# Spreading weight preparation over the steps of a Strassen matmul kernel, and loading the first rows as whole 128-row tiles

## The chip, the cores and the metric

The kernel runs on one core of one Trainium2 chip. The metric is device time in microseconds (us), median over the runs of one kernel.

## The reference, cut to what matters

Two layers of attention over a graph. Each multiplies the tokens `h` by three 768 x 768 matrices (left, right, lin) of that layer:

```python
h = jnp.maximum(_layernorm(x, axis=-1), 0.0)
for l in range(L):                                   # L = 2
    m_left  = jnp.einsum('bsh,oh->bso', h, W_left[l])
    m_right = jnp.einsum('bsh,oh->bso', h, W_right[l])
    u_left  = jnp.einsum('bih,bjh->bij', h, m_left) / temper
    u_right = jnp.einsum('bih,bjh->bij', h, m_right) / temper
    ...                                              # masked exp of u, rows normalized: attention
    h_lin = jnp.einsum('bsh,oh->bso', h, W_lin[l]) + b_lin[l]
    ctx = jnp.matmul(attention, h_lin)
    h = jax.nn.relu(_layer_norm(ctx, ln_a[l], ln_b[l]))
return x + h
```

`x` is 128 x 64 x 768 in float32: 16 blocks of 512 tokens.

## The kernel before

Each layer is two passes over the 16 blocks. The first computes left, right and the attention ("scores"), the second lin and the context. The products are Strassen's: seven in place of eight, with sums of weight quarters (S1 to S4) and of token quarters (T1 to T4) prepared by VectorE or GpSimd. One product is a *step*: three float32 matmuls, which the trace shows as six, into one of the PSUM banks X, Y, Z and V, the tiles that matmuls write and that VectorE or ScalarE then reads. In the profiles, ts are the token sums, wm the masks or (beside w_n) its means, and aux takes the transposes of the first rows, the scores and the context. A block of the first pass is 42 steps and one group of scores.

Every other engine's work is put into a queue, and one item is taken after each step. So a place in the queue is a place in time, and an empty item (a "blank") moves all that follows by one step. The order on each engine is fixed when the program is built. Cuts are marked with "..."; some short lines are joined.

```python
queue = deque()
def pump(n):
    for _ in range(min(n, len(queue))):
        queue.popleft()()

def centre(l):                       # subtract the column mean from w_n ("lin")
    ...
        queue.append(means)          # four VectorE operations on w_n and a 128x3 tile
        for s in (a, b):
            queue.append(lambda s=s, m=m: nc.gpsimd.tensor_sub(t[s], t[s], ...))

def sums_w(l, kind, eng):            # S1..S4 of one matrix
    ...
        queue.append(lambda ...: getattr(eng, f)(t[o], t[a], t[b]))

def load_rows(l, u, pool, engines=(nc.sync, nc.sync)):
    for g in range(2):
        t = pool.tile([P, 2, H], F32, name="x", bufs=2)
        for a in range(4):           # eight pieces of 32 partitions
            ...
            engines[a % 2].dma_start(t[a * 32:(a + 1) * 32], src.rearrange("(k j) h -> j k h", k=2))

def prepare(u):                      # what block u needs, queued while block u-1 is multiplied
    transpose_rows(l, u, sp)
    queue.append(lambda: load_h(1, l, u))
    if u + 1 < NB:
        queue.append(lambda: load_rows(l, u + 1, sp))
    queue.extend(softmax(u - 2) if u > 1 else [lambda: None] * 6)
    queue.append(lambda: load_adj(u))
    queue.extend([lambda: None] * 6)
    affine(1, l, u)                  # layer 1 only: six ScalarE operations on ht
    queue.append(lambda: masks(u))   # GpSimd, needs adj
    sums_t((1, l, u))                # GpSimd: T1..T4

# pass one, layer 0, before block 0
warm = const.tile(...); nc.scalar.activation(warm, eps_in, AF.Sqrt)   # among the constants
load_rows(0, 0, sp, (nc.sync, nc.scalar)); load_w(0, "l"); load_w(0, "r")
...
sums_w(0, "l", nc.vector)            # interleaved with T1..T4 on VectorE
sums_w(0, "r", nc.gpsimd)
...
for u in range(NB):
    if u == 0:
        queue.extend([lambda: None] * 9)
    ...

def one_aside(l):                    # begun after the first third of a block-1 matrix
    ...                              # in an inner function:
    load_w(l, "n"); bias(l); centre(l); sums_w(l, "n", nc.gpsimd)
```

`bias(l)` loads two rows of `b_lin` and queues six VectorE operations on them (`centred`).

## Time and profile before

| | before |
|---|---|
| median, lowest to highest (6 runs) | 2971.37, 2970.22 to 2975.54 us |
| span of the profiled run | 2970.2 us |
| TensorE busy | 2910.5 us, 98% |
| TensorE idle, all | 59.7 us |

TensorE sets the time: only what it waits for can be won. This is the timeline of the kernel before (start, duration, engine, line, operation, out<-in, count, and in brackets the idle time and what ended it; ACTq is ScalarE's queue of DMA issues):

```profile
0.73 1.28 ACT L163 ACT_TABLE_LOAD   x1 [0.73 <-PEq L654]
...
1.39 0.86 ACTq L189 DMA_DIRECT2D x<-in_x_dram  x2
...
4.53 3.70 ACTq L189 DMA_DIRECT2D x<-in_x_dram  x2
...
14.36 1.02 DVE L175 BATCH_NORM_STATS2 st<-x 128x6 f32<-128x384 f32 x2 [4.42 <-DMA x<-in_x_dram]
```

ScalarE issues two of its four pieces of x at once and the other two only from 4.53 us on. The second half of x is there at 14.36, and the first product waits for it.

### The profile page before, as it was taken

What the parts mean: (1) busy time and instruction counts of PE and PEld (TensorE: products, weight loads), DVE (VectorE), ACT (ScalarE), POOL (GpSimd) and SP (SyncE); (2) the same over time, 40 slices, a digit from 0 to 9 for tenths busy, and PEclk for the clock granted to TensorE, in tenths of its full rate; (3) what the DMA queues carried; (4) which work ended last, traced back from release to release, by engine and by line L of the source; (5) the groups of instructions that cost most, each with busy time, mean ns of one, the idle gap of its engine ahead of it and who ended that gap; (6) DMA issues with size and microseconds to landing.
All of it is one profiled execution on the core that took longest, in us unless ns stands there. A gap on an engine that the chain in (4) does not pass through costs nothing.

```text
span 2970.2 us, 37457 instructions
## 1 busy us (share of the span) xinstructions
PE 2910.5 (98%) x14872; PEld 2246.1 (76%) x14872; DVE 1130.0 (38%) x2312; ACT 582.6 (20%) x1113; POOL 768.2 (26%) x482
## 2 busy tenths in 40 slices
PE   6989999999999999999999999999999999999998
PEld 5878888888888755555588888888888886555554
DVE  5433443334333332222334332333333324555555
ACT  2111211121111122222221111111111112232221
POOL 2132111211121152323223111111111113656564
PEclk9999999999999999999999999999999999999999
DMA  5522234223422153333453342234223303555544
GB/s 152 152 70 70 70 97 108 73 70 91 113 74 70 39 177 101 120 100 121 124 131 107 93 112 73 70 90 114 75 70 83 101 27 114 165 163 149 174 143 133
DMA packets 228719, 310.23 MB, mean 104 GB/s; under 512 B 53696, under 2 KB 179136, under 8 KB 220352
## 3 DMA queue, kind: packets, MB, share of 16 engines
q1 hardware_dynamic: 228224, 307.05, 37.3%
q8 instruction: 117, 1.92, 0.3%
q10 hardware_dynamic: 320, 0.79, 0.1%
q14 instruction: 58, 0.48, 0.1%
HBM read 202.91 MB, written 104.86 MB: 104 GB/s over the span
## 4 chain that ended last, share of the span: by engine, by line
PE 93%; DMA 3%; POOL 2%; SPq 1%; DVE 1%; issue 0%; ACT 0%; DVEq 0%; POOLq 0%; ACTq 0%
PE V L310 16%; PE Z L310 16%; PE X L310 16%; PE Z L543 8%; PE V L543 8%; PE X L543 8%; PE Y L310 8%; PE aux L344 5%; PE Y L543 5%; PE aux L471 3%; DMA x<-in_x_dram 1%; DMA h<-xb 1%; POOL w_n_A L110 1%; POOL w_n_S L118 1%; POOL ts L141 0%; DMA adj<-in_adj_dram 0%
## 5 line engine op out<-in xcount | busy, mean ns | idle before, releaser
L280 POOL TENSOR_TENSOR wm<-adj,tri 128x256 f32<-128x256 f32 x64 | 46.9, 754 | 1401.3 <-DMA adj<-in_adj_dram 1269.7
L141 POOL TENSOR_TENSOR ts<-ht 128x768 f32<-128x768 f32 x126 | 240.0, 1905 | 278.5 <-PE Y L310 157.2
L310 PE MATMUL V<-ts,w_l_A 128*128 128x256 f32 x1152 | 284.4, 383 | 15.3 <-POOL ts L141 11.2
L310 PE MATMUL V<-ts,w_r_A 128*128 128x256 f32 x1152 | 281.4, 380 | 2.2 <-DVE n L331 2.2
L310 PE MATMUL X<-ht,w_l_A 128*128 128x256 f32 x1152 | 282.8, 382 | 0.0
L310 PE MATMUL X<-ht,w_r_A 128*128 128x256 f32 x1152 | 280.3, 379 | 0.0
L543 PE MATMUL X<-w_n_A,ht 128*128 128x384 f32 x768 | 268.8, 486 | 0.0
L543 PE MATMUL V<-w_n_A,ts 128*128 128x384 f32 x768 | 268.6, 486 | 0.0
L329 ACT COPY n<-X 128x256 f32<-128x256 f32 x192 | 71.4, 372 | 1003.9 <-PE X L310 1003.9
L331 DVE TENSOR_TENSOR n<-V,u 128x256 f32<-128x256 f32 x384 | 161.9, 422 | 251.8 <-PE V L310 251.3
L310 PEld LDWEIGHTS V<-ts,w_l_A 128*128 128x128 f32 x1152 | 221.0, 192 | 46.9 <-POOL ts L141 12.0
L310 PEld LDWEIGHTS X<-ht,w_l_A 128*128 128x128 f32 x1152 | 220.9, 192 | 31.2 <-issue 0.6
L310 PEld LDWEIGHTS V<-ts,w_r_A 128*128 128x128 f32 x1152 | 219.6, 191 | 32.5 <-DVE n L331 2.6
L310 PEld LDWEIGHTS X<-ht,w_r_A 128*128 128x128 f32 x1152 | 219.3, 190 | 29.9
L141 POOL TENSOR_TENSOR ts<-ht,ts 128x768 f32<-128x768 f32 x126 | 238.6, 1894 | 5.8 <-issue 3.3
L543 PEld LDWEIGHTS V<-w_n_A,ts 128*128 128x128 f32 x768 | 145.9, 190 | 101.8
L543 PEld LDWEIGHTS X<-w_n_A,ht 128*128 128x128 f32 x768 | 145.8, 190 | 101.6 <-issue 0.3
L497 ACT ACTIVATE z<-aux 128x768 f32<-128x768 f32 x128 | 102.5, 806 | 601.0 <-PE aux L471 586.9
L324 DVE TENSOR_TENSOR u<-Y,s 128x256 f32<-128x256 f32 x192 | 81.6, 425 | 363.3 <-PE Y L310 359.4
L331 DVE TENSOR_TENSOR n<-Z,u 128x256 f32<-128x256 f32 x192 | 81.3, 424 | 306.9 <-PE Z L310 306.8
L327 DVE TENSOR_TENSOR u<-Z,u 128x256 f32<-128x256 f32 x192 | 81.5, 425 | 285.8 <-PE Z L310 285.2
L553 POOL TENSOR_TENSOR u2b<-u,b 128x384 f32<-128x384 f32 x64 | 63.8, 997 | 478.5 <-DVE u L551 465.1
(103 smaller groups left out, 4004.1 us busy)
## 6 DMA issues: line engine op xcount, KB each, us to landing
ht<-h SPq DMA_DIRECT2D x63, 1536.0 KB, 7.1
h<-xb SPq DMA_DIRECT2D x124, 384.0 KB, 6.0
z<-z SPq DMA_DIRECT2D x128, 192.0 KB, 2.9
x<-z SPq DMA_DIRECT2D x128, 192.0 KB, 8.7
xr<-in_x_dram SPq DMA_DIRECT2D x128, 192.0 KB, 3.3
out_dram<-xr SPq DMA_DIRECT2D x128, 192.0 KB, 2.7
x<-in_x_dram SPq DMA_DIRECT2D x124, 192.0 KB, 8.6
adj<-in_adj_dram SPq DMA_DIRECT2D x64, 128.0 KB, 2.8
```

The source lines that it names most:

```text
L141: eng.tensor_sub(b[o], b[m], b[n])
L280: nc.gpsimd.tensor_tensor(WM[u][:, :, k], ADJ[u][:, :, 1 - k], t, op=ALU.mult)
L310: nc.tensor.matmul(p, w[a][:, c, g * P:(g + 1) * P], b[t][:, c, :], start=(new and c == 0), stop=(c == CH - 1), skip_group_check=True)
L324: nc.vector.tensor_add(u2, p, s1)
L327: nc.vector.tensor_add(u4, p, u2)
L329: nc.scalar.copy(to, pb)
L331: nc.vector.tensor_add(to, pb, (u4 if i == 3 else u2).rearrange("p (b s) -> p b s", s=S))
L344: nc.tensor.matmul(p[h * S:(h + 1) * S, q, :], ht[:, c, b * S:(b + 1) * S], m[c // CH][:, c % CH, b].rearrange("p k j -> p (k j)"), start= ...
L471: nc.tensor.matmul(cx[k][i, m, :HH], at[j, q, :], hl[j, q, m * HH:(m + 1) * HH], start=True, stop=True)
L497: nc.scalar.activation(zs[k].rearrange(two, n=2), cx[k], AF.Square, accum_out=ss[:, k:k + 1])
L543: nc.tensor.matmul(p, b[t][:, c, r * P:(r + 1) * P], w[a][:, c, :], start=(new and c == 0), stop=(c == CH - 1), skip_group_check=True)
L553: nc.gpsimd.tensor_add(u2b, u2, rows["b2"])
```

## The change

It is meant to remove the waits of TensorE outside the first loads. A second queue, `idle`, is drawn on only in steps where the first has nothing or a blank. The preparation of w_n goes there, with two blanks ahead of each item, so that token sums on GpSimd come first. The sums of w_r go to VectorE during block 0. The first x is loaded as four whole 128-row tiles ahead of the warming square root.

```diff
+    idle = deque()
+    none = [None]
     def pump(n):
-        for _ in range(min(n, len(queue))):
-            queue.popleft()()
+        for _ in range(n):
+            f = queue.popleft() if queue else None
+            if f is None and idle:
+                f = idle.popleft()
+            if f is not None:
+                f()
 ... in centre: means and tensor_sub
-            queue.append(means)
+            idle.append(means)             # each with idle.extend(none * 2) ahead of it
 ... in bias
-        queue.append(centred)
+        idle.append(centred)
 ... in load_rows, for the first block
+            for g in range(2):
+                t = pool.tile([P, 2, H], F32, name="x", bufs=2)
+                for k in range(2):
+                    engines[k].dma_start(t[:, k, :], rows[0, 2 * g + k])
 ... in prepare
-                queue.extend(softmax(u - 2) if u > 1 else [lambda: None] * 6)
+                queue.extend(softmax(u - 2) if u > 1 else [])
 ... in pass one
-    nc.scalar.activation(warm, eps_in, AF.Sqrt)          # among the constants
                 load_rows(0, 0, sp, (nc.sync, nc.scalar))
+                nc.scalar.activation(warm, eps_in, AF.Sqrt)
-                sums_w(0, "r", nc.gpsimd)
                 if u == 0:
-                    queue.extend([lambda: None] * 9)
+                    queue.extend(none * 4)
+                    if l == 0:
+                        sums_w(0, "r", nc.vector, queue, 1)   # a blank ahead of each
+                    else:
+                        queue.extend(none * 5)
 ... in one_aside
-            sums_w(l, "n", nc.gpsimd)
+            sums_w(l, "n", nc.gpsimd, idle, 2)
```

Left out here: the first rows' new order of tokens in the copy to ht, a loop that empties `idle` after the last block of a pass, and the same blanks written in another way in the second pass.

More of the change, by code (lines that the diff above doesn't have):

```diff
@@ L73, with flush @@
     queue = deque()
+    idle = deque()
+    none = [None]
     def pump(n):
-        for _ in range(min(n, len(queue))):
-            queue.popleft()()
-    def flush(keep=0):
-        pump(len(queue) - keep)
+        for _ in range(n):
[4 more added lines that the diff above has]
+                f()
+    def flush():
+        while queue:
+            pump(1)
     SRC = {"l": w_left, "r": w_right, "n": w_lin}
@@ L100, in centre @@
             m = stat.tile([P, 2, CH], F32, name="wm", bufs=2)
+            idle.extend(none * 2)
             def means(a=a, b=b, m=m):
@@ L106, in means, with sums_w @@
                 nc.vector.tensor_scalar_mul(m[:, 0], m[:, 0], 1.0 / H)
-            queue.append(means)
+            idle.append(means)
             for s in (a, b):
-                queue.append(lambda s=s, m=m: nc.gpsimd.tensor_sub(
+                idle.extend(none * 2)
+                idle.append(lambda s=s, m=m: nc.gpsimd.tensor_sub(
                     t[s], t[s], m[:, 0].unsqueeze(2).to_broadcast([P, CH, HH])))
-    def sums_w(l, kind, eng):
+    def sums_w(l, kind, eng, to, apart=0):
         t = W[l, kind]
@@ L117, in sums_w @@
                            ("S3", "tensor_sub", "A11", "S3"), ("S4", "tensor_sub", "A12", "S2")):
-            queue.append(lambda o=o, f=f, a=a, b=b: getattr(eng, f)(t[o], t[a], t[b]))
+            to.extend(none * apart)
+            to.append(lambda o=o, f=f, a=a, b=b: getattr(eng, f)(t[o], t[a], t[b]))
     ORDER = (("X", "A11", "B11"), ("Y", "S2", "T2"), ("Z", "S1", "T1"), ("V", "S3", "T3"),
@@ L161 @@
     nc.gpsimd.memset(floor, 1e-30)
-    warm = const.tile([P, 1], F32, name="warm")
-    nc.scalar.activation(warm, eps_in, AF.Sqrt)
     diff = const.tile([P, S], I32, name="diff")
@@ L183, in load_rows @@
         XR[l, u] = []
+        if (l, u) == (0, 0):
+            rows = x.rearrange("(n k h) s f -> n k (h s) f", k=Q, h=PAIR)
+            for g in range(2):
+                t = pool.tile([P, 2, H], F32, name="x", bufs=2)
+                for k in range(2):
+                    engines[k].dma_start(t[:, k, :], rows[0, 2 * g + k])
+                    XR[l, u].append(t[:, k, :])
+            return
         for g in range(2):
@@ L188, in load_rows @@
                 src = x[u * NBB + i] if l == 0 else ROWS[u][i]
-                engines[a % 2].dma_start(t[a * 32:(a + 1) * 32], src.rearrange("(k j) h -> j k h", k=2))
+                nc.sync.dma_start(t[a * 32:(a + 1) * 32], src.rearrange("(k j) h -> j k h", k=2))
             XR[l, u].extend([t[:, 0, :], t[:, 1, :]])
@@ L243, in turn @@
                 for c in range(2):
-                    nc.scalar.copy(ht[:, c0 + c, :].rearrange("p (a q j) -> p q a j", a=4, q=Q),
-                                   p[:, c].rearrange("p (q a j) -> p q a j", a=4, q=Q))
+                    nc.scalar.copy(ht[:, c0 + c, :].rearrange("p (a g s) -> p g a s", a=4, g=2),
+                                   p[:, c].rearrange("p (g a s) -> p g a s", a=4, g=2))
             for c in range(0, C, 2):
@@ L290, in prepare @@
                     queue.append(lambda: load_rows(l, u + 1, sp))
-                queue.extend(softmax(u - 2) if u > 1 else [lambda: None] * 6)
+                queue.extend(softmax(u - 2) if u > 1 else [])
                 queue.append(lambda: load_adj(u))
-                queue.extend([lambda: None] * 6)
+                queue.extend(none * 6)
                 affine(1, l, u)
@@ L379, in pass_one @@
                 load_rows(0, 0, sp, (nc.sync, nc.scalar))
+                warm = stat.tile([P, 1], F32, name="warm", bufs=1)
+                nc.scalar.activation(warm, eps_in, AF.Sqrt)
                 load_w(0, "l")
@@ L386, in pass_one @@
                 tokens = [queue.popleft() for _ in range(4)]
-                sums_w(0, "l", nc.vector)
+                sums_w(0, "l", nc.vector, queue)
                 sums = [queue.popleft() for _ in range(4)]
                 queue.extend(sums[:2] + tokens[:2] + [sums[2], tokens[2], sums[3], tokens[3]])
-                sums_w(0, "r", nc.gpsimd)
             load_adj(0)
@@ L402, in pass_one @@
                 else:
-                    queue.extend([lambda: None] * 6)
+                    queue.extend(none * 6)
                     queue.append(lambda: load_h(2, l, 0))
-                    queue.extend(softmax(u - 1) + [lambda: None] * 4)
+                    queue.extend(softmax(u - 1) + none * 4)
                     affine(2, l, 0)
@@ L416, in pass_one @@
                             flush()
-                            queue.extend([lambda: None] * 3 + late)
+                            queue.extend(none * 3 + late)
                 flush()
@@ L421, in pass_one @@
             flush()
+            while idle:
+                pump(1)
     rows = {}
@@ L568, in linear @@
                         pump(1)
-                    if aside:
-                        aside.popleft()()
+                    f = aside.popleft() if aside else None
+                    if f:
+                        f()
             load(0)
@@ L580, in pass_two @@
                     beside = deque()
-                    nop = [lambda: None]
                     turn = not last and u >= NB - 2
@@ L586, in pass_two @@
                             if u:
-                                queue.extend(nop * 4)
+                                queue.extend(none * 4)
                                 affine(2, l, u + 1, 2)
@@ L592, in pass_two @@
                             queue.append(lambda: load_h(1, 1, 0))
-                        queue.extend(nop * (7 - len(queue)))
+                        queue.extend(none * (7 - len(queue)))
                         if u in aside:
@@ L611, in pass_two @@
                     linear(u, r, before, beside)
-                    while beside:
-                        beside.popleft()()
+                    for f in beside:
+                        if f:
+                            f()
             finish(NB - 1, 1)
@@ L627, in begin @@
             load_w(1, kind)
-            return lambda: sums_w(1, kind, nc.gpsimd)
+            return lambda: sums_w(1, kind, nc.gpsimd, queue)
         return begin
```

## The prediction

> **What bounds the kernel now.** I read the page first, then TensorE's waits, then the timelines of the places where it waited.
>
> ```profile
> PE 2910.5 (98%) x14872; PEld 2246.1 (76%) x14872; DVE 1130.0 (38%) x2312; ACT 582.6 (20%) x1113; POOL 768.2 (26%) x482
> ```
>
> TensorE is busy for 2910.5 of 2970.2 us, so only 59.7 us are idle. The change leaves the matmuls alone: the instruction orders of the two programs are identical on TensorE, shape by shape. Two per cent would be 59.4 us, practically all the idle time. What can be won lies in these waits (total, times, longest):
>
> ```profile
> PE V L310 <- POOL ts L141: 11.2, 2, 9.0
> PE aux L241 <- DMA x<-in_x_dram: 11.1, 1, 11.1
> PE aux L241 <- ACT x L222: 7.7, 3, 5.4
> PE Y L310 <- POOL ts L141: 5.1, 1, 5.1
> PE V L310 <- DVE ts L141: 4.1, 1, 4.1
> PE Y L310 <- DVE ts L141: 2.9, 1, 2.9
> PE V L310 <- DVE n L331: 2.2, 1, 2.2
> PE Z L310 <- DVE u L327: 0.8, 1, 0.8
> ```
>
> Where they fall: the aux and DVE ts waits are the start of layer 0 (before 36 us); Y <- POOL is block 1 (95.0); the 9.0 is block 2 (175.1); the other 2.2 of POOL (1631) and the 2.2 of DVE n (1607) are blocks 2 and 1 of layer 1. TensorE around the longest (start, us, group):
>
> ```profile
> 164.55 1.56 PE L310 MATMUL Z<-ts,w_l_S 128*128 128x256 f32 x6
> 175.13 2.93 PE L310 MATMUL V<-ts,w_l_A 128*128 128x256 f32 x6 [9.02 <-POOL ts L141]
> 177.85 2.71 PE L310 MATMUL X<-ht,w_l_A 128*128 128x256 f32 x6
> 180.40 1.46 PE L310 MATMUL Z<-ht,w_l_S 128*128 128x256 f32 x6
> ```
>
> Steps of six matmuls normally start 1.295 us apart. From Z at 164.55 to V would be 1.40; it is 10.58. V and X after the pause then take 2.72 and 2.55. A pause thus costs its length plus a slow restart: here 9.18 + 1.43 + 1.25 = 11.9. GpSimd in that time:
>
> ```profile
> 152.72 1.81 POOL L141 TENSOR_TENSOR ts<-ht,ts 128x768 f32<-128x768 f32 x1
> 154.49 8.30 POOL L110 TENSOR_TENSOR w_n_A<-w_n_A,wm 128x1152 f32<-128x1152 f32 x4
> ...
> 173.28 1.80 POOL L141 TENSOR_TENSOR ts<-ht 128x768 f32<-128x768 f32 x1
> ```
>
> Eight preparations of w_n (8.3 us of centring, four sums of 2.6) sit between the second token sum and the third, which V needs.
>
> **What the Trainium skill says.** "TensorE: Matmul & The Clock Gate", Part 1, says the array falls to half clock after an idle window of about 3.4 us and recovers after about as long a busy one. The trace agrees on the slow restart (2.93 against 1.46 us a group), but shows it after a pause of only 2.18 us too; I use the measured extras, 1.7 to 2.7 us a pause. "SBUF — State Buffer", Who interferes with whom: a VectorE instruction with two SBUF inputs and a GpSimd one that reads SBUF lock each other out. The trace agrees: a w_l sum took 1.36 us at 20.43, begun before GpSimd's, and 3.77 at 28.32 beside GpSimd's w_r sums; token sums took 3.00 and 3.36 against 1.18. The same page, The DMA port swizzle: partitions 0..31 reach 8 of 16 ports. The trace agrees: 223 to 286 GB/s while 32-partition pieces of x led (2 to 7 us), 371 to 374 when 128-partition weights loaded alone (14 to 20 us). And the clock-gate page's first table has ScalarE's and VectorE's queues strictly first in, first out: an instruction that waits for data holds up everything behind it. That matters most below.
>
> **The change part by part.**
>
> *Start of layer 0 (-15.0).* Now the second half of x lands only at 14.2 us, because ScalarE's third and fourth issues wait for earlier landings; the last normalization ends at 20.19. With four 384 KB loads, two a queue, all issued first, I estimate x in by 5.2 (first pair) and 8 us (second), from the 350 to 370 GB/s above plus the observed 2 us before data flows. Then statistics (1.24), root (0.29), two small VectorE operations (0.33) and normalization (1.03), at the 1.64 us pitch seen now at 15.88, 17.52 and 19.16, end the fourth normalization near 13.8: 6.4 us sooner. The ht copies end at 25.37 - 6.4 = 19.0. With GpSimd's w_r sums gone, T2 takes about 1.0: Y starts near 20.0, not 28.45. S3 (1.36) and T3 (1.0) finish at 22.4, just before V's turn at 22.6; it started at 35.42, cold. Behind S4, T4 and VectorE's first reads, the second Z starts near 25.65 against 40.7. Gain 15.0.
>
> *Block 1 of layer 0 (+4.8).* The four w_r sums and their blanks fill 8 slots after 4 blanks, where 9 blanks stood: preparation of block 1 starts 3 steps later. VectorE's last transpose now goes behind V of step 25: in the old frame it ends at 67.97, not 63.67. From there to T2 runs a chain of DMAs (store, reload, x, adjacency) and GpSimd, 63.67 to 94.96, untouched: 31.3 us. So Y's wait grows by 4.3 to 9.4, with a slower restart 4.8 in all.
>
> *Block 2 of layer 0 (-11.9 - 1.0).* GpSimd's new order is masks, T1, T2, two centrings (4.2), T3, T4. T3 ends near 154.5 + 4.2 + 1.8 = 160.5; V asks at 166. The pause goes. The two groups of means are no longer neighbours on VectorE, so the 0.8 us Z pause with its restart goes too.
>
> *Layer 1, block 0 (+4.9).* `softmax(u-2) if u > 1 else []` drops six blanks in block 0, which moves the six ScalarE affines of block 1's ht from step 30 to step 24. They wait for a DMA:
>
> ```profile
> 1531.33 0.34 SPq L194 DMA_DIRECT2D ht<-h x1
> 1538.89 2.22 ACT L201 ACTIVATE ht<-ht,b_col,a_col 128x512 f32<-128x512 f32 x3
> ```
>
> These loads take 7.3 to 7.7 us, so this one is there at about 1538.7. At step 24 (1531.9) ScalarE will wait, and the X copy of step 26 stands behind the first two affines: free near 1540.5. TensorE wants that bank at step 29, 1537.3. A new pause of 3.2 plus 1.7.
>
> *Layer 1, block 1 (+20.7).* The largest term, and one that the diff alone hides. The bias preparation now leads the idle list, and takes the first blank: step 15 of block 1. In the static order VectorE's reduction of b stands ahead of the Y addition of step 16, with a wait for b's load. VectorE around that reduction before:
>
> ```profile
> 1599.95 0.42 DVE L324 TENSOR_TENSOR u<-Y,s 128x256 f32<-128x256 f32 x1 [2.22 <-PE Y L310]
> 1600.51 0.55 DVE L437 TENSOR_REDUCE bm<-b 128x1 f32<-128x384 f32 x1
> 1601.11 0.55 DVE L438 TENSOR_REDUCE bm<-b 128x1 f32<-128x384 f32 x1
> ```
>
> The two b loads are issued at 1590.1 and 1590.9 and take 10.1 to 10.4 us: they land when it starts, at step 30. Nothing moves them, since the sync queue's order is the same. Step 15 ends near 1580.3, so VectorE will be stuck for some 20 us. TensorE runs on until step 20, where Z needs the bank of step 17's Z, unread: from 1585.4. VectorE is free after the six bias operations at 1603.0, reads Y and Z by 1603.9. Pause 18.5, restart 2.2. (In layer 0 the same reduction comes at step 24, long after b landed near 97 us.)
>
> *The old pauses of layer 1 (-8.2).* The means in a row (2.18) and the GpSimd one (2.17) go; each also had 0.16 of spacing and 1.74 of restart: 4.08 each.
>
> Sum: -15.0 + 4.8 - 11.9 - 1.0 + 4.9 + 20.7 - 8.2 = -5.7 us; 2971.5 - 5.7 = 2965.8, rounded to 2966.
>
> **The rivals.** (1) The intended result: no new pause, all pauses outside the first loads go. Then -15.0 - 7.0 - 11.9 - 1.0 - 8.2 = -43, or 2928. For it: every wait named in the change's words is in the list. Against it: the order on VectorE and the landing of b contradict it; it needs b some 20 us sooner. (2) Half of that: the late b costs nothing because VectorE was not needed, while block 1 still waits. 2966 - 20.7 is about 2945. Against it: only one tile per PSUM name is allocated, and Z comes round after three steps (3.9 us). (3) The start gains nothing, because weights share the DMA engines with x and land as late as before: S1 and S2 ran at 19.0 to 21.8 without a DMA wait. If w_l came only then, T2 would still lose its GpSimd collision, and the gain falls to some 9: 2972. Against it: x and w_l are 3.9 MB, 11 us at 360 GB/s. (4) GpSimd becomes the bound: at 26% busy, with T3 done 5 us early, no.
>
> **Range and chances.** The start may be off by 2 to 3 us, block 1 by 1.5, the two new pauses by 3 each, the base by 2: together about 6. A pause I have not seen would add, an overlooked slack subtract. I say 2956 to 2975. Faster by 2% needs 2912, below the intended result; slower by 2% needs 3031, another 65 us of pauses. Within 2% has 0.98.
>
> **What would show it.** Right: a TensorE wait of about 18 us on Z near 1567 (1585.4 less the 18.2 gained by then), released by VectorE's addition, with the bias reduction waiting for the b load just before; a wait of about 3 us on X, released by ScalarE's copy, near 1514; Y of block 1 waiting about 9 us for GpSimd; no wait of V on POOL; the first Y near 20 us; x landed by 8 us. Wrong: b landing before step 15 (then some 20 us better), affines that find their ht, or first matmuls still after 28 us.

## The result, and the profile after

| | before | after |
|---|---|---|
| median, lowest to highest (6 runs each) | 2971.37, 2970.22 to 2975.54 | 2968.59, 2967.13 to 2969.90 us |
| span of the profiled run | 2970.2 | 2965.4 us |

The ratio is 0.9988, with a 95% interval of 0.9976 to 1.0001: the same within 2%. The ratios are not quite the ratios of the medians quoted.

First the busy times, from the page of the changed kernel, then its list of TensorE's waits (total, times, longest):

```profile
PE 2906.3 (98%) x14872; PEld 2243.7 (76%) x14872; DVE 1128.6 (38%) x2316; ACT 582.6 (20%) x1113; POOL 754.4 (25%) x478
```

```profile
PE Z L326 <- DVE u L343: 17.4, 2, 16.7
PE aux L257 <- ACT x L239: 12.6, 4, 9.2
PE Y L326 <- POOL ts L151: 9.0, 1, 9.0
PE X L326 <- ACT n L345: 2.9, 1, 2.9
PE aux L360 <- DVE n L347: 1.7, 1, 1.7
PE Y L326 <- DVE ts L151: 1.0, 1, 1.0
PE aux L494 <- DMA at<-att: 0.5, 1, 0.5
```

The waits of V for POOL (11.2), for DVE ts (4.1) and for DVE n (2.2) are gone. In their place stand one of 16.7 for Z, one of 2.9 for X and one of 1.7 for aux, the scores; and Y's wait for POOL has grown from 5.1 to 9.0.

Since the order on TensorE is the same, a landmark can be compared in both timelines. These are the starts of the first Y, of block 0's second Z, of each block's scores, and of the last context group:

| landmark | before | after | after - before | new in this stretch |
|---|---|---|---|---|
| first Y | 28.45 | 20.11 | -8.34 | |
| block 0, second Z | 40.57 | 25.39 | -15.18 | -6.84 |
| scores of block 0 (in block 1's steps) | 97.87 | 86.62 | -11.25 | +3.93 |
| scores of block 1 | 159.16 | 147.48 | -11.68 | -0.43 |
| scores of block 2 | 230.99 | 209.34 | -21.65 | -9.97 |
| layer 1, scores of block 0 | 1557.93 | 1540.89 | -17.04 | +4.61 |
| layer 1, scores of block 1 | 1621.99 | 1621.29 | -0.70 | +16.34 |
| layer 1, scores of block 2 | 1686.04 | 1681.26 | -4.78 | -4.08 |
| last context group | 2953.93 | 2949.11 | -4.82 | -0.04 |

From block 2 on, layer 0 runs 21.65 us earlier. Two blocks at the start of layer 1 give nearly all of it back. There TensorE's timeline of the changed kernel is:

```profile
1567.11 1.46 PE L326 MATMUL X<-ht,w_l_A 128*128 128x256 f32 x6
1585.25 2.93 PE L326 MATMUL Z<-ht,w_l_S 128*128 128x256 f32 x6 [16.69 <-DVE u L343]
1587.97 2.62 PE L326 MATMUL V<-ts,w_l_A 128*128 128x256 f32 x6
```

VectorE's, in the same time, and the issue of b's two loads:

```profile
1562.13 0.42 DVE L347 TENSOR_TENSOR n<-V,u 128x256 f32<-128x256 f32 x1 [0.52 <-PE V L326]
1582.01 0.55 DVE L460 TENSOR_REDUCE bm<-b 128x1 f32<-128x384 f32 x1 [19.45 <-DMA b<-in_b_lin_dram]
...
1584.25 0.42 DVE L340 TENSOR_TENSOR u<-Y,s 128x256 f32<-128x256 f32 x1
```

```profile
1572.85 1.19 SPq L450 DMA_DIRECT2D b<-in_b_lin_dram  x2
```

VectorE does nothing from 1562.5 to 1582.0. The bias reduction stands ahead in its order and waits for a load that is issued only at 1572.85. Nothing that stood behind it ran in those 19.45 us, so the trace agrees with the strict order, first in, first out, that the prediction takes from the skill. The addition that frees Z's bank stands behind it. In block 0 of that layer, ScalarE does the same on a smaller scale:

```profile
1516.46 1.52 ACT L218 ACTIVATE ht<-ht,b_col,a_col 128x512 f32<-128x512 f32 x2 [8.41 <-DMA ht<-h]
1517.89 0.35 ACT L345 COPY n<-X 128x256 f32<-128x256 f32 x1
```

The copy that frees X's bank comes after two affines that waited 8.41 us for ht; TensorE lost 2.87 us there and restarted slowly.

The wait of 1.7 us was not foreseen. It is in block 2's preparation in layer 0. VectorE, then GpSimd, in the changed kernel:

```profile
146.68 1.62 DVE L113 TENSOR_TENSOR wm<-wm 128x3 f32<-128x3 f32 x1
148.34 1.74 DVE L114 TENSOR_SCALAR wm<-wm 128x3 f32<-128x3 f32 x1
```

```profile
144.11 4.17 POOL L119 TENSOR_TENSOR w_n_A<-w_n_A,wm 128x1152 f32<-128x1152 f32 x2
148.24 1.80 POOL L151 TENSOR_TENSOR ts<-ht 128x768 f32<-128x768 f32 x1
```

These belong to the second group of means. In the kernel before, the same two operations were:

```profile
151.49 1.17 DVE L105 TENSOR_TENSOR wm<-wm 128x3 f32<-128x3 f32 x1
152.69 0.17 DVE L106 TENSOR_SCALAR wm<-wm 128x3 f32<-128x3 f32 x1
```

With no GpSimd work beside them, those of the first group took 0.16 and 0.17 us, before (148.24) as after (128.55). Now the first of the second group ends at 148.30, GpSimd's second centring at 148.28; the second ends at 150.08, the token sum at 150.04. Each tiny operation lasts until the GpSimd instruction beside it is over. The addition for the scores stands behind both.

### The profile page after: what moved, and what is told of

Same layout as the page of the kernel before. It is cut to its first block, busy times and chain, and to the rows that moved or that the text cites. A ratio compares the mean times of both kernels' runs of the same rounds, so it can differ in the third digit from the quotient of the medians.

```text
span 2965.4 us, 37443 instructions
## 1 busy us (share of the span) xinstructions
PE 2906.3 (98%) x14872; PEld 2243.7 (76%) x14872; DVE 1128.6 (38%) x2316; ACT 582.6 (20%) x1113; POOL 754.4 (25%) x478
## 4 chain that ended last, share of the span: by engine, by line
PE 94%; DMA 3%; DVE 1%; SPq 1%; issue 0%; ACT 0%; POOL 0%; DVEq 0%; ACTq 0%; POOLq 0%
PE Z L326 16%; PE V L326 16%; PE X L326 16%; PE Z L566 8%; PE V L566 8%; PE X L566 8%; PE Y L326 8%; PE aux L360 6%; PE Y L566 5%; PE aux L494 3%; DMA h<-xb 1%; DMA x<-z 1%; DMA x<-in_x_dram 0%; DMA b<-in_b_lin_dram 0%; SPq L273 0%
## 5 line engine op out<-in xcount | busy, mean ns | idle before, releaser
L337 ACT COPY s<-X 128x256 f32<-128x256 f32 x192 | 71.1, 370 | 587.0 <-PE X L326 586.9
```

The costliest lines, as they stand in the source:

```text
L337: nc.scalar.copy(s1, p)
```

## The experiments

All experiments are edits of the changed kernel, three rounds each, all correct. They ran in three groups, each on one chip: the first four beside before at 2973.50 (7 runs), the next four beside 2970.62 (7), the last three beside 2970.89 (8). A row's ratio is to before in the same group; the changed kernel stood at 0.9988. It was run again only in the last group, as e11. Before differs by up to 2.9 us between groups, so a gain worked out below against 2968.59 is uncertain by some 2 to 3 us; the waits in the traces are the firmer measure.

| run | median us | ratio, 95% interval |
|---|---|---|
| e1_bias_back | 2962.27 | 0.9961 (0.9944 to 0.9977) |
| e2_idle_late | 2945.07 | 0.9906 (0.9891 to 0.9921) |
| e3_blanks_back | 2964.24 | 0.9969 (0.9954 to 0.9983) |
| e4_sums_close | 2963.75 | 0.9968 (0.9953 to 0.9983) |
| e5_rows_old | 2970.62 | 1.0000 (0.9983 to 1.0017) |
| e6_gpsimd_sums | 2972.71 | 1.0007 (0.9992 to 1.0022) |
| e7_all_three | 2936.69 | 0.9887 (0.9872 to 0.9902) |
| e8_adj_first | 2929.55 | 0.9861 (0.9846 to 0.9876) |
| e9_rows_old_warm_first | 2974.87 | 1.0015 (0.9998 to 1.0031) |
| e10_warm_first | 2968.31 | 0.9993 (0.9978 to 1.0008) |
| e11_unchanged | 2968.68 | 0.9992 (0.9975 to 1.0008) |

### e1_bias_back: the bias back in the first queue

```diff
-        idle.append(centred)
+        queue.append(centred)
```

> Only the bias preparation goes back to the main queue; the means stay in the idle list. Theory A (whatever VectorE meets first that needs a late DMA holds the line): the first group of means moves up to step 17 of block 1 in layer 1 and waits for w_n there, which lands some 3 to 4 us before b; the pause of 16.7 us shrinks to about 11 on V instead of Z, 5.5 us faster: 2963. Theory B (the bias reduction alone is the cause): the pause goes, some 19 us faster: 2949.

Measured: 2962.27, ratio 0.9961. Of VectorE's timeline and of TensorE's waits in this run:

```profile
1578.85 1.35 DVE L111 TENSOR_REDUCE wm<-w_n_A 128x3 f32<-128x1152 f32 x1 [11.75 <-DMA w_n_A<-in_w_lin_dram]
```

```profile
PE V L326 <- DVE n L347: 11.9, 1, 11.9
```

The bias no longer waits, but the first operation of the idle queue is now the means of w_n, whose load lands almost as late. The wait has another name and is 11.9 us long: theory A. So the fault is not the bias as such, but that the idle queue starts before its data are there.

### e2_idle_late: six blanks at the head of the idle queue

```diff
             load_w(l, "n")
+            idle.extend(none * 6)
             bias(l)
```

> Six more blanks at the head of each idle list, so that nothing of it runs before step 30 of block 1 in layer 1. Theory A: b and w_n have landed by then, the 16.7 us pause and its slow restart go, 19 to 20 us faster: 2949. Rival (the pause only moves, for instance to GpSimd or to the adjacency load of block 2, since nothing else has been sped up): less than 5 us faster, and a new wait of 10 us or more in the list.

Measured: 2945.07, ratio 0.9906. TensorE's waits:

```profile
PE aux L257 <- ACT x L239: 12.3, 4, 8.9
PE Y L326 <- POOL ts L151: 9.7, 1, 9.7
PE X L326 <- ACT n L345: 2.2, 1, 2.2
```

The wait for Z is gone with no other in its place, and so are the two small ones, 1.7 at the scores and 0.7 at Z, which the shifted means avoid. By the traces the Z pause with its restart is worth 19.4 us and the two small ones some 2.9, together 22.3 of the 23.5 us between the medians; the two small ones are most of the 4 us by which the expectation of 2949 was missed. It also settles the rival "the late b costs nothing": it cost more than any single gain of the change.

### e3_blanks_back: the six blanks of `prepare` in block 0 and 1

```diff
-                queue.extend(softmax(u - 2) if u > 1 else [])
+                queue.extend(softmax(u - 2) if u > 1 else none * 6)
```

> The six blanks of block 0 back, so that the affines stand at steps 30 to 35 again. Theory: the wait of X for ScalarE (2.9 us, with 0.2 of spacing and 1.8 of slow restart) goes: 4.8 us faster, 2964, and nothing else changes. Rival (the later b wait absorbs it, since b lands at a fixed time): same time as the changed kernel, with the b wait longer by 4.8.

Measured: 2964.24, ratio 0.9969, as expected. X's wait for ScalarE is not in the list any more; Z (17.8) and Y (9.8) stay. The dropped blanks alone made that pause.

### e4_sums_close: the sums of w_r without blanks between them

```diff
-                        sums_w(0, "r", nc.vector, queue, 1)
+                        sums_w(0, "r", nc.vector, queue)
+                        queue.extend(none)
```

The preparation of block 1 then starts in the same step as in the kernel before.

> The four w_r sums on VectorE without blanks between them and one blank behind: 9 slots as before, so the rows of block 1 start 3 steps earlier. Theory: Y of block 1 waits about 5 us instead of 9.0, 4 to 4.5 us faster: 2964. Rival (VectorE falls behind when the sums are back to back, or x of block 1 has not landed): Y still waits 7 us or more, or new small waits on Z and V appear in block 0.

Measured: 2963.75, ratio 0.9968. Of TensorE's waits:

```profile
PE Y L326 <- POOL ts L151: 5.2, 1, 5.2
```

It is back at the 5.1 of before, and block 0 shows no new wait. The spacing of those sums bought nothing and cost about 4.8 us.

### e5_rows_old: eight pieces of 32 partitions again

```diff
-        if (l, u) == (0, 0):
+        if False:
 ...
-                nc.sync.dma_start(t[a * 32:(a + 1) * 32], src...)
+                engines[a % 2].dma_start(t[a * 32:(a + 1) * 32], src...)
 ... and the copy's layout of before, (p a q j)
```

> The changed kernel with the first rows loaded as before, in eight pieces of 32 partitions. Theory: the last normalization ends some 6.4 us later again and everything behind it moves by that: 6 us slower than the changed kernel, 2975; first Y near 26 us, and no wait of V for VectorE beside it. Rival 1 (the whole 15 us of the start come from the loads): 15 us slower, 2984. Rival 2 (the loads don't matter, w_l lands late anyway): same time.

Measured: 2970.62, ratio 1.0000: 3.6 us slower than the changed kernel by the ratios (0.0012 x 2971), and 1.9 slower than e11, the changed kernel on the same chip, by the medians, where about 6 was expected. A miss. The timeline shows why:

```profile
0.73 1.85 ACTq L206 DMA_DIRECT2D x<-in_x_dram  x4
...
10.97 1.02 DVE L183 BATCH_NORM_STATS2 st<-x 128x6 f32<-128x384 f32 x2 [1.18 <-DMA x<-in_x_dram]
```

All four of ScalarE's issues go out from 0.73 us on, and the second half of x is there at 10.97 instead of 14.36. The edit had left the warming square root behind the loads. Part of the gain at the start was thus not the shape of the pieces, which e9 and e10 take up.

### e6_gpsimd_sums: the sums of w_r back on GpSimd

```diff
                 queue.extend(sums[:2] + tokens[:2] + [sums[2], tokens[2], sums[3], tokens[3]])
+                sums_w(0, "r", nc.gpsimd, queue)
 ...
-                    if l == 0:
-                        sums_w(0, "r", nc.vector, queue, 1)
-                    else:
-                        queue.extend(none * 5)
+                    queue.extend(none * 5)
```

> The changed kernel with the w_r sums on GpSimd before block 0, as before, and nine blanks in block 0. Theory: VectorE's sums collide with GpSimd's, the first V waits 4 to 6 us more and restarts slowly, some 9 us lost at the start; block 1 gets its 3 steps back, 4.5 gained: 4 to 5 us slower than the changed kernel, 2973. Rival (VectorE's operations don't get longer beside GpSimd's now that w_r lands at another time): 4.5 us faster, 2964.

Measured: 2972.71, ratio 1.0007, as expected. VectorE's timeline of this run, and below it that of the changed kernel:

```profile
21.70 3.77 DVE L128 TENSOR_TENSOR w_l_A<-w_l_A,w_l_A 128x1152 f32<-128x1152 f32 x1
25.39 3.36 DVE L151 TENSOR_TENSOR ts<-ht 128x768 f32<-128x768 f32 x1
```

```profile
19.97 1.35 DVE L128 TENSOR_TENSOR w_l_A<-w_l_A,w_l_A 128x1152 f32<-128x1152 f32 x1
21.24 0.95 DVE L151 TENSOR_TENSOR ts<-ht 128x768 f32<-128x768 f32 x1
```

The same sums take 3.77 and 3.36 us with GpSimd beside them, 1.35 and 0.95 without. V waited 4.1 us for them again, and block 0's second Z started at 34.76 instead of 25.53 in e11. Y of block 1 waited 5.0, as in the kernel before.

### e7_all_three: e2, e3 and e4 together

> The idle lists late, the six blanks back and the w_r sums close together, all at once. Theory (the three losses are separate pauses that add up): the 2945 of the late idle list, less 3 to 5 for X on ScalarE and 4 to 5 for Y of block 1: 2937. Rival (they share their time): above 2942.

Measured: 2936.69, ratio 0.9887, 1.1% below before. TensorE's waits:

```profile
PE aux L257 <- ACT x L239: 12.6, 4, 9.2
PE Y L326 <- POOL ts L151: 4.8, 1, 4.8
PE Y L326 <- DVE ts L151: 1.0, 1, 1.0
```

The three repairs add up: 23.5 + 4.4 + 4.8 by the medians from 2968.59 gives 2935.9. (By the ratios it would be 36 us in sum against 30 measured, which is within their intervals.) The list has nothing left but the first loads, block 1's Y and 0.7 us before a context group.

### e8_adj_first: e7, and block 1's adjacency loaded ahead of block 2's rows

```diff
                 queue.append(lambda: load_h(1, l, u))
+                if u == 1:
+                    queue.append(lambda: load_adj(u))
                 if u + 1 < NB:
                     queue.append(lambda: load_rows(l, u + 1, sp))
 ...
-                queue.append(lambda: load_adj(u))
+                queue.append((lambda: load_adj(u)) if u > 1 else None)
```

> As e7, and in block 0 of both layers the adjacency of block 1 is loaded ahead of the rows of block 2. Theory: the masks of block 1 stand first on GpSimd and wait for this load; it lands some 6 us sooner, so the 5.2 us wait of Y in block 1 goes with its slow restart: 7 us faster than e7, 2930. Rival (T2 waits for ht, which lands just before, or the rows of block 2 now come late and hold VectorE): gain under 3 us, with Y still waiting or a new wait on VectorE in block 1.

Measured: 2929.55, ratio 0.9861, 1.4% below before: faster than both kernels. GpSimd's first instruction for block 1, and TensorE's waits:

```profile
68.60 1.42 POOL L296 TENSOR_TENSOR wm<-adj,tri 128x256 f32<-128x256 f32 x2 [38.59 <-DMA adj<-in_adj_dram]
```

```profile
PE aux L257 <- ACT x L239: 12.4, 4, 9.0
PE Z L328 <- DVE n L349: 0.4, 1, 0.4
PE aux L497 <- DMA at<-att: 0.4, 1, 0.4
PE Y L328 <- DVE ts L151: 0.3, 1, 0.3
```

The changed kernel's masks started at 78.67. With them, and so the token sums, ten microseconds earlier (some four of them from e4's edit), block 1's Y does not wait at all. What remains is nearly all the time until the first rows are in.

### e9_rows_old_warm_first, e10_warm_first, e11_unchanged: what the start's loads gained, and from what

```diff
 e9: the edits of e5, and; e10: this alone
     nc.gpsimd.memset(floor, 1e-30)
+    warm = const.tile([P, 1], F32, name="warm")
+    nc.scalar.activation(warm, eps_in, AF.Sqrt)
 ...
                 load_rows(0, 0, sp, (nc.sync, nc.scalar))
-                warm = stat.tile([P, 1], F32, name="warm", bufs=1)
-                nc.scalar.activation(warm, eps_in, AF.Sqrt)
```

> Eight 32-partition pieces as in the run with the old rows, and the warming square root ahead of ScalarE's loads again, as in the kernel before. Theory A (the loading gain is two things: about 3.6 us the shape of the pieces, about 2.7 us that the warming no longer stands ahead of ScalarE's loads): ScalarE's third and fourth load issues wait for earlier landings again, the third statistics start near 14.4 instead of 10.97, the first Y lies near 26.4 instead of 23.75, and the time is 2.7 us above the run with the old rows alone, about 6.3 above the changed kernel. Theory B (the warming's place does not matter, the pieces' shape alone made the difference of 3.5): the third statistics stay near 11, Y near 23.7, and the time is 3.5 above the changed kernel.

> The changed kernel with the warming ahead of ScalarE's loads: its two loads are issued about 0.7 us later, and the order of the issues makes the second of them wait for the landing of the first 128-row tile (near 5.3). Theory A: the last tile of x then goes out beside the weights and lands some 2 to 4 us later than it did, so the fourth statistics, which started at 9.52, start 1 to 3 us later and the first Y is at 21 to 23 instead of 20.11; the time is 1 to 3 us above the unchanged kernel. Theory B: there is slack, the fourth statistics stay within 0.5 us, and the time is within 0.5 us of the unchanged kernel.

> The changed kernel with no edit, beside these two on the same chip, as their base: 2968.6 give or take 1.5, a ratio near 0.9988; first Y at 20.1. All theories say the same of it.

Measured: e9 2974.87 and e11 2968.68, 6.2 apart; e10 2968.31, within 0.4 of e11. The timeline of e9:

```profile
4.34 3.57 ACTq L208 DMA_DIRECT2D x<-in_x_dram  x2
...
14.06 1.02 DVE L185 BATCH_NORM_STATS2 st<-x 128x6 f32<-128x384 f32 x2 [4.43 <-DMA x<-in_x_dram]
```

This is the picture of the kernel before: the last two issues late, the second half of x at 14.06. The first Y starts at 26.83 in e9, 23.75 in e5 and 20.24 in e11. So with 32-partition pieces the place of the warming is worth 3.1 us at the first Y, and the shape of the pieces another 3.5. Theory A holds for e9.

For e10 the two theories split: the fourth statistics start at 10.13 instead of 9.38 and Y at 21.27 instead of 20.24, within what A said of Y. ScalarE's second load was issued at 3.92 us, just when the first tile's statistics could start, so it did wait for that landing. But the time is that of B. The profiles suggest where the microsecond went: the wait for the scores of block 1 was 0.4 us in e10 and 1.9 in e11. With the warming first, VectorE's and GpSimd's small collision fell differently, which is seen in e10, then in e11:

```profile
148.53 0.16 DVE L113 TENSOR_TENSOR wm<-wm 128x3 f32<-128x3 f32 x1
148.73 1.97 DVE L114 TENSOR_SCALAR wm<-wm 128x3 f32<-128x3 f32 x1
```

```profile
147.30 1.88 DVE L113 TENSOR_TENSOR wm<-wm 128x3 f32<-128x3 f32 x1
149.21 1.73 DVE L114 TENSOR_SCALAR wm<-wm 128x3 f32<-128x3 f32 x1
```

In e10 the first operation fell between two of GpSimd's centrings and took 0.16 us. That this offset is more than chance is not shown: one profile each, and a difference of medians below what three rounds resolve.

## Why the prediction was right

The range held and the class was right. But the range, 19 us wide, also holds the time of before, so the waits that were named test the prediction better than the time does. The predicted sum was -5.7 us; the profiled runs differ by 4.8, the medians by 2.8. The profiled run of after was the fastest of its six. In the control e11, of the same program, the Z pause was 17.8 and the pause at the scores 1.9 us, against 16.7 and 1.7: 1.3 of the 2.0 us between the two differences. It is partly luck that the sum came so close: 2.9 us of collisions that were not foreseen stand against a pause for b that was 1.3 us shorter than predicted and four smaller errors of the same sign. Step by step, with the landmarks of the table:

- **Start of layer 0: -15.0 predicted, -15.2 measured.** Right in the sum and in its stages: the last normalization ended at 13.94 (predicted 13.8), Y started at 20.11 (20.0), the second Z at 25.39 (25.65). For the second Z of before the prediction read 40.7, the trace has 40.57. The last piece of x had landed by 7.5 us (8 was estimated); the transfers moved 403 GB/s from 4 to 8 us, better than the 350 to 370 assumed, and 220 in e5 with the 32-partition pieces. What the prediction put down to loading as a whole proved to be two causes: shape of pieces, and place of the warming (e5, e9). The rest of the gain is VectorE without GpSimd beside it (9.2 us at the second Z, e6 against e11).
- **Block 1 of layer 0: +4.8, measured +4.55** (3.93 up to the scores, and scores that then took 6.34 us, 0.62 longer than before). Y's wait was 9.0, predicted 9.4. e4 shows the cause, the blanks between the w_r sums.
- **Block 2: -11.9 and -1.0; measured -9.97 and -1.05** (the latter is -0.43 less the 0.62 of the line above). V does not wait, as predicted. The shortfall of 1.9 is the step that failed: "the two groups of means are no longer neighbours on VectorE" is true, but the second group now runs beside GpSimd's centring and token sum, and its two tiny operations, 1.17 and 0.17 us before, became 1.62 and 1.74, with the addition that the scores need behind them. The prediction had applied the collision to large sums alone. The trace of before already held the sign: the 1.17 us at 151.49 end with GpSimd's token sum.
- **Layer 1, block 0: +4.9, measured +4.61.** The pause of X was 2.87 at 1518 instead of 3.2 near 1514; e3 shows that the dropped blanks made it.
- **Layer 1, block 1: +20.7, measured some 19.4.** From X at 1567.11 to Z at 1585.25 it is 18.14 instead of 1.295, and V and X after it started 1.43 and 1.17 late: 16.85 + 2.60 = 19.4. The mechanism was right, and e2 removes it. The size was off in one term, the landing of b: 8.8 to 9.1 us after issue in the trace, not the 10.1 to 10.4 taken from before. In the same stretch the old 4.08 left and a second unforeseen pause of 0.70 (Z at 1615.91) came, again behind the means beside GpSimd: 19.4 - 4.1 + 0.9 = 16.2, against the table's 16.34.
- **The old pauses of layer 1: -8.2, measured -4.08** for the one that stands alone in a stretch; the other is inside the line above.

Of the rivals, "half of that", 2945, is what e2 measured (2945.07); that it agrees to the microsecond is luck, since e2 also lost the two small pauses that no rival knew of. "The intended result", 2928, was reached within 2 us by e8, with a fourth repair that the change did not attempt. So the change did remove most of the old waits (that of Y in block 1 grew); most of what they were worth went into new ones, behind ScalarE and VectorE, which are 20% and 38% busy.

Open: why the pause of Z varied between 16.7 and 17.8 us for one program, and why b landed sooner than before. Something goes with the latter. From 14 to 16 us, when weights load alone, the profiles of before, e9 and e10 moved 373 to 375 GB/s, and the ten others 398 to 403; in the loads of w_n in layer 1 it is some 373 against some 400 again. Those three are the runs with the warming square root ahead of ScalarE's loads, and e10 differs from e11 (373 against 403) in nothing else. Why its place should matter for later loads no run shows, nor that this is all of the difference in b: in e8 b took 10.0 to 10.6 us at the higher rate.

## What to carry to other kernels

Work that is moved to "idle" slots of an in-order engine is free only once its data are there: before advancing an operation, look up when its load lands, since a low busy share says nothing of what stands behind the operation in the engine's order. Empty steps in a hand-made schedule may be holding a load's latency, so ask of each what waits behind it before deleting it. A large change that moves the time little is best read by landmarks of the engine that sets the time: the stretches where the gain is given back name the repair, and here three small edits turned 0.1% into 1.1%.

## What the Trainium skill lacked or had wrong

- "TensorE: Matmul & The Clock Gate", Part 1: it ties the slow restart to an idle window of about 3.4 us. The runs show slow groups after shorter pauses too: 2.62 and 2.13 us in place of 1.46 after a pause of 2.87 us at 1518.29 in the changed kernel, and 2.18 in the kernel before; but after 2.23 us in e2 the next group took 1.56 and the one after it 1.46. Of the eleven pauses of 2.17 to 3.00 us ahead of products in the 13 profiles, eight were followed by slow groups and three (2.23 in e2, 2.36 in e5, 2.53 in e10) were not, so the length alone does not decide. Part 1 speaks of shorter pauses only as "micro-idles", without a length.
- "SBUF — State Buffer", Who interferes with whom: the rule that the later instruction blocks for the whole of the earlier one agrees with the runs, but no size is given for tiny operations, where it matters most for a chain. A 128x3 operation of 0.16 us took up to 1.97 us beside GpSimd in the changed kernel, e10 and e11, and ended within 0.04 us of the GpSimd instruction. This holds for the tensor_scalar too, while a reduction of 128x1152 beside the same instructions stayed at 1.34, both as that section has it.
- No page has a rate of loads that differs with the place of one ScalarE operation ahead of the first loads and still differs in layer 1: 373 GB/s in e10 against 403 in e11, from 14 to 16 us.
